# Keys and the second layer's first product from quarters, values ahead of the queries, channel sums in node order

## The chip, the core and the metric

The kernel runs on one core of a Trainium2 chip. The metric is the device time of one execution in microseconds (us): the median of several runs. Five engines work side by side[...]: TensorE multiplies matrices (PE in the profile, its weight loads PEld), VectorE (DVE) and ScalarE (ACT) do elementwise work, GpSimd (POOL) does some elementwise work and issues part of the DMAs, and SyncE (SP) issues the other DMAs. Each engine works through its own instructions in program order.

## The reference

Two layers over 16 graphs of N = 1024 nodes with C = 256 channels each, all in float32. `LN` is a layer normalisation over the channels.

```
# layer 0, per graph, h = relu(LN(x))
c      = mean over channels of h                         # one number per node
A      = | |sigmoid(c[m] - c[n]) - 0.5| - 0.5 | * 2      # N x N, symmetric
g      = relu((h^T @ (adj * A)) * para)                  # C x N
q      = g^T in 4 heads of 64;   k, v = h @ kv_w in 4 heads
x      = x + softmax(q k^T * scale) v
# layer 1, h = relu(LN(x))
agg    = D (adj + I) D h                                 # D from the degrees
y      = agg @ W1^T + b1                                 # 256 -> 512 channels
z      = relu(batchnorm(y)) @ W2^T + b2                  # batchnorm over all graphs and nodes
x      = x + batchnorm(z)
```

The first batch norm needs `y` of all graphs, so the kernel has two phases: everything up to `y` graph by graph, with `y` stored in DRAM, and after that the second product and the second batch norm.

## The kernel before

**Layout.** Channels or nodes lie on the 128 partitions. N is 8 tiles of 128 (`NT`), C is 2 (`CC`), the 512 channels of `y` are 4 (`HC`), and a product writes 128 x 512 (`FB`). `product` (lines 167 to 171) makes one 128 x 128 by 128 x 512 product from two matmuls with 64 columns each, which the trace shows as four records. It is the line L171 of queries, keys, values, aggregate and `hidden` alike, which differ by the tile they write: `pg`, `pk`, `pv`, `pa`, `py`.

**Attention sets the beat.** `attention` (from line 1092) walks through 16 graphs, 4 units each (two pairs of heads, two halves of the queries), 4 steps per unit: 256 steps. A step issues the scores of two key tiles (`sc`, L933), their exponentials (`p`, L941, ScalarE), the additions of `p` for the softmax's denominator (`acc`, L962 and L965, VectorE) and the products with the values (`o`, L976) of the step before. When a unit ends, VectorE transposes `o` (L990), GpSimd writes it to `out_d` (L994), SP reads it back (`gather`, L1000), VectorE folds `acc` (L1011, L1012), and a few steps later `add_output` (L1074, L1082) scales the result and adds it to `xs[b]`, the residual.

**The background.** Between the steps, `background(b)` hands out the other graphs' work in pieces. Each piece yields its TensorE time in us; `attention` takes pieces until the sum reaches `due`, a share of `total` that grows evenly over the graph's 16 steps. While graph b attends, the background makes, in this order: keys and values of graph b+1 (`keys_values`: 8 products of keys from `ht`, copied out by ScalarE at L660, then 4 banks of values, copied out at L677); the queries of b+1 (`queries`, seven products of quarters in place of eight, with `weigh` making the weights, and `normed(b-1)` the second norm of the graph before, which ends with `load_x(b + 2)` for its freed buffer); the aggregate of b-1 (`aggregate`, again seven products of quarters), with the first norm of b+2 beside it; and `hidden(b-1)`: 8 blocks of two products each, biased and copied by ScalarE (L773), written to DRAM by GpSimd (L774), their statistics taken by VectorE (L777). `prepare(b+2)` weaves into `hidden` the transposed copy of graph b+2's `h` (`squares` on VectorE, written to `hsq_d`, read back by `gathered`) and the first weights. An action given to `soon` is issued with the next piece.

**Seven for eight.** `queries`, `aggregate` and the second phase use a scheme for 2 x 2 blocks that takes seven products and 15 block additions. The second operand's combinations in order are t1 = b12 - b11, t2 = b22 - t1, t3 = b22 - b12, t4 = b21 - t2; the first's are s1 = a21 + a22, s2 = s1 - a11, s3 = a11 - a21, s4 = a12 - s2.

**Buffers.** Products of the background share three PSUM banks in rotation (`ps_mm`, through `bank`); `o` has one bank, `sc` two tiles. Pool `p4` has four buffers of `p`, `p3` three each of `x`, `ht` and `adj`, `p2` two of `h`, `p8` eight weights, `py` four of `y`.

**Channel sums.** `weigh` needs c for every node twice: per partition (`csum`) and along the row (`cbc`, the same row on all partitions). `differences` (from line 428) writes `csum` to `csum_d` and reads it back to all partitions. For graph 0 and 1 the row is in node order. From graph 2 on it is written as it lies, (partition, tile), and `weigh` reads it with a step of 8 elements: `cbc.rearrange("p (q t) -> p t q", t=NT)`. The reader is L485, `w<-cbc,csum`.

**The degrees' row.** `load_later` (lines 290 to 297), called once in graph 1's background, loads W1, writes `dinv` to `dinv_d` (L294) and reads it back to all partitions as `dbc` (L295); `aggregate` scales with it.

Of the kernel before, what the change touches and what calls it, by code (L numbers as in the profile page):

```python
# [10 lines left out]
F32 = mybir.dt.float32  # L11
# [12 lines left out]
def gnn_two_layers_kernel(  # L24
# [34 lines left out]
    vec = const.tile([P, 18], F32, name="vec")  # L59
    nc.sync.dma_start(out=vec, in_=vecs)  # L60
    b1, g1, be1 = (vec[:, i * HC : (i + 1) * HC] for i in range(3))
    b2, g2, be2 = (vec[:, 3 * HC + i * CC : 3 * HC + (i + 1) * CC] for i in range(3))
# [34 lines left out]
    def layers(shifted):  # L97
# [13 lines left out]
        py = st.enter_context(tc.tile_pool(name=f"py_{kind}", bufs=4))  # L111
# [7 lines left out]

        xs, hs, hts, ats, qs, ks, vs = {}, {}, {}, {}, {}, {}, {}  # L120
        invs = {}
        csums, cbcs, weighted, weighers = {}, {}, {}, {}
# [50 lines left out]
        def load_x(b):  # L173
            xs[b] = p3.tile([P, NT, C], F32, tag="x", name=f"x_{b}")
            parts = 4 if b == 0 else 2
            for part in range(parts):
                t = slice(part * NT // parts, (part + 1) * NT // parts)
                nc.sync.dma_start(
                    out=xs[b][:, t], in_=x[b].rearrange("(t p) c -> p t c", p=P)[:, t]
                )  # L180
# [108 lines left out]

        def load_later():  # L290
            later["w1"] = big.tile([P, CC, H1], F32, tag="w1", name="w1")
            nc.sync.dma_start(out=later["w1"], in_=w1_t.rearrange("(k p) j -> p k j", p=P))
            later["dbc"] = const.tile([P, N], F32, tag="dbc", name=f"dbc_{kind}")
# [5 lines left out]
        class Norm:  # L299
# [3 lines left out]
            def __init__(self, b, first):  # L303
                tag = "a" if first else "b"
                self.src = xs[b]
# [4 lines left out]
                if first:  # L310
                    self.csum = p2.tile([P, NT], F32, tag="csum", name=f"csum_{b}")
                    csums[b] = self.csum
                self.h = p2.tile([P, NT, C], F32, tag="h", name=f"h_{tag}_{b}")
# [114 lines left out]
        def differences(b):  # L428
# [4 lines left out]
            cbcs[b] = (  # L433
                cbc.rearrange("p (t q) -> p t q", t=NT)
                if b <= 1
                else cbc.rearrange("p (q t) -> p t q", t=NT)
            )
# [4 lines left out]
            if b == 1:  # L442
                turned = bank(f"csumt_{b}")[0:NT, 0:P]
                nc.tensor.transpose(turned, csums[b], ident)
                row = p1.tile([P, NT // 2, P], F32, tag="s1", name=f"csumr_{b}")[0:NT, 0, :]
                nc.scalar.copy(row, turned)
                nc.sync.dma_start(out=csum_d[b].rearrange("(t p) -> t p", p=P), in_=row)
            else:
                nc.sync.dma_start(out=csum_d[b].rearrange("(p t) -> p t", p=P), in_=csums[b])
# [199 lines left out]
        def keys_values(b):  # L649
            ht = hts[b]  # L650
            ks[b] = [p4.tile([P, N], F32, tag="k", name=f"k_{b}_{k}") for k in range(CC)]
            for g in range(NH):
                for j in range(CC):
# [7 lines left out]
                    yield 1.71  # L661

            vs[b] = [p4.tile([P, NT, P], F32, tag="v", name=f"v_{b}_{k}") for k in range(CC)]
# [18 lines left out]
        def aggregate(b):  # L682
# [3 lines left out]
            order = (0, 2, 5, 1, 4, 6, 3)  # L686
# [35 lines left out]
            def sixth(m):  # L722
                add(c21, m, c21)
                soon(lambda: scale(c21, 0))
# [5 lines left out]
            for i, (left, after) in enumerate(  # L730
# [5 lines left out]
                    (None, fifth),  # L736
                    (a22, sixth),
                    (a12, seventh),
# [4 lines left out]
                for th in range(NP // 2):  # L743
# [9 lines left out]
                    elif i == 0:  # L753
                        combine("b", b, nc.vector)
                    yield 1.71

        def hidden(b):

# [31 lines left out]
        def normed(b):  # L790
# [4 lines left out]
            if b + 3 < B:  # L795
                load_x(b + 3)
# [15 lines left out]
        def prepare(b, products):  # L812
# [4 lines left out]
            if b == 2:  # L817
                for k in range(CC):
                    yield from weave(islice(products, 3), (0, islice(w, AHEAD // 2)))
                    yield TOP  # L820
                    transposed(b, (k,))
                    yield 1.0
# [741 lines left out]
```

## Time and profile before

| what | us |
|---|---|
| median of 3 runs | 2489.23 (2488.91 to 2490.34) |
| the profiled execution | 2488.76 |
| its span | 2487.0 |
| granted TensorE clock over the span | 0.993 |

An engine's "busy" is the union of its instructions' times. "x" gives how many there were. In a row of windows, the first numbers are the stretch from the span's start, its length, and then each engine's busy time with the instructions in brackets; at the end come the granted TensorE clock, the share that the DMA engines were busy, and GB/s. A row of waits names the instruction that waited, what released it, the total in us, how often, and the longest. In a timeline a row has its start, its length, the engine, the line, the operation, out<-in with shapes, and how many in a row; in brackets is the idle time ahead of it. The rows of the groups that the change concerns:

```profile
L485 ACT ACTIVATE w<-cbc,csum 128x512 f32<-128x512 f32 x256 | 285.8, 1168 | 0.0
L171 PE MATMUL py<-at,w 128*64 128x512 f32 x1024 | 228.4, 592 | 0.2 <-ACT y L773 0.2
L773 ACT ACTIVATE y<-py,vec 128x512 f32<-128x512 f32 x128 | 87.4, 683 | 115.4 <-PE py L171 91.8
L171 PE MATMUL pk<-ht,kvw_f 128*64 128x512 f32 x512 | 115.2, 592 | 0.2 <-ACT ht L404 0.2
```

The stages: until about 75 us the first graph's own preparation, until 2160 the attention with its background, until 2214 the last aggregate and `hidden`, then the second phase.

### The profile page before, as it was taken

The page shows a single profiled execution, that of the slowest core. Times are in us where ns is not written, and L with a number is a line of the kernel's source. Part 1 is how long each engine was busy: PE and PEld are TensorE (multiplying, and loading weights), DVE is VectorE, ACT ScalarE, POOL GpSimd, SP SyncE. Part 2 cuts the span into 40 slices and gives each one's busy share as a digit, 9 for nine tenths or more (in the row PEclk, how much of TensorE's full clock was granted, in tenths as well). Part 3 has the DMA queues.
Part 4 walks back from the last instruction along what each step waited for, and adds up shares of the span by engine and source line. Part 5 has one row for each costly group of instructions (what it writes and reads, how often), then busy time and mean ns, then how long its engine had stood idle before and what let it go on. Part 6 is the DMA issues. An engine that isn't in the chain of part 4 may idle for free. (4 is left out here: it accounts for less than half of the span.)

```text
span 2487.0 us, 35569 instructions
## 1 busy us (share of the span) xinstructions
PE 2435.7 (98%) x13403; PEld 841.2 (34%) x13403; DVE 1882.0 (76%) x2920; ACT 1401.7 (56%) x1927; POOL 429.2 (17%) x527
## 2 busy tenths in 40 slices
PE   9999999999999999999999999999999999999995
PEld 4333333333333333333333333333333332334444
DVE  5668787877778787878787787868787877767775
ACT  7775564647473746656474747465564634345544
POOL 1640101010101001011101010110101001036652
PEclk9999999999999999999999999999999999999997
DMA  4754535354545545362645445543536344355559
GB/s 150 238 173 172 170 114 199 101 199 129 197 145 178 164 159 169 116 206 84 215 126 182 145 174 169 178 153 132 191 94 210 116 140 162 132 214 220 189 199 374
DMA packets 187909, 421.42 MB, mean 169 GB/s; under 512 B 21832, under 2 KB 81744, under 8 KB 181968
## 3 DMA queue, kind: packets, MB, share of 16 engines
q1 hardware_dynamic: 158560, 311.56, 37.9%
q0 software_dynamic: 29168, 107.50, 11.6%
q8 instruction: 108, 1.77, 0.3%
q14 instruction: 73, 0.60, 0.1%
HBM read 315.63 MB, written 103.35 MB: 168 GB/s over the span
## 5 line engine op out<-in xcount | busy, mean ns | idle before, releaser
L941 ACT ACTIVATE p<-sc 128x1024 f32<-128x1024 f32 x512 | 494.9, 1019 | 617.6 <-PE sc L933 617.2
L965 DVE TENSOR_TENSOR acc<-acc,p 128x1024 f32<-128x1024 f32 x384 | 471.3, 1227 | 165.1 <-ACT p L941 143.8
L933 PE MATMUL sc<-q,k 64*64 64x512 f32 x4096 | 498.8, 602 | 6.2 <-ACT p L941 6.2
L976 PE MATMUL o<-p,v 128*64 128x512 f32 x2048 | 494.5, 604 | 0.3 <-DVE os L990 0.3
L171 PE MATMUL pg<-w,h_a 128*64 128x512 f32 x1600 | 359.8, 592 | 0.8 <-DVE w L472 0.8
L171 PE MATMUL pa<-aht,h_b 128*64 128x512 f32 x1536 | 346.0, 592 | 1.1 <-ACT h_b L342 1.0
L485 ACT ACTIVATE w<-cbc,csum 128x512 f32<-128x512 f32 x256 | 285.8, 1168 | 0.0
L933 PEld LDWEIGHTS sc<-q,k 64*64 64x64 f32 x4096 | 131.0, 132 | 347.9 <-issue 286.5
L472 DVE SCALAR_TENSOR_TENSOR w<-w,adj 128x1024 f32<-128x1024 f32 x128 | 156.9, 1225 | 95.0 <-ACT w L493 91.1
L171 PE MATMUL py<-at,w 128*64 128x512 f32 x1024 | 228.4, 592 | 0.2 <-ACT y L773 0.2
L976 PEld LDWEIGHTS o<-p,v 128*64 128x64 f32 x2048 | 124.4, 136 | 298.3 <-issue 260.3
L994 POOL DMA_DIRECT2D out_d<-os x58 | 34.2, 590 | 1070.8 <-DVE os L990 1037.5
L171 PEld LDWEIGHTS pg<-w,h_a 128*64 128x64 f32 x1600 | 114.8, 137 | 229.2 <-issue 218.8
L171 PEld LDWEIGHTS pa<-aht,h_b 128*64 128x64 f32 x1536 | 109.9, 137 | 215.3 <-issue 202.0
L773 ACT ACTIVATE y<-py,vec 128x512 f32<-128x512 f32 x128 | 87.4, 683 | 115.4 <-PE py L171 91.8
L493 ACT ACTIVATE w<-w 128x1024 f32<-128x1024 f32 x128 | 135.1, 1055 | 1.7
L774 POOL DMA_DIRECT2D y_d<-y x128 | 69.7, 545 | 371.8 <-ACT y L773 362.6
L548 DVE TENSOR_TENSOR w<-w,w 128x1024 f32<-128x1024 f32 x112 | 132.7, 1214 | 1.5
L171 PEld LDWEIGHTS py<-at,w 128*64 128x64 f32 x1024 | 74.0, 137 | 145.5 <-issue 131.5
L171 PE MATMUL pv<-kvw_f,ht 128*64 128x256 f32 x1024 | 116.1, 379 | 0.0
L171 PE MATMUL pk<-ht,kvw_f 128*64 128x512 f32 x512 | 115.2, 592 | 0.2 <-ACT ht L404 0.2
L342 ACT ACTIVATE h_b<-x,lnsm_b 128x256 f32<-128x256 f32 x128 | 69.9, 599 | 65.9 <-DVE lnsm_b L331 65.9
(169 smaller groups left out, 2665.4 us busy)
## 6 DMA issues: line engine op xcount, KB each, us to landing
aht<-aht_d SPq DMA_DIRECT2D x224, 512.0 KB, 6.4
adj<-in_adj_dram SPq DMA_DIRECT2D x128, 512.0 KB, 4.8
y_d<-y POOLq DMA_DIRECT2D x128, 256.0 KB, 3.0
yin_f<-y_d SPq DMA_DIRECT2D x32, 1024.0 KB, 6.4
para<-in_para_dram SPq DMA_DIRECT2D x64, 256.0 KB, 3.6
x_d<-x POOLq DMA_DIRECT2D x16, 1024.0 KB, 5.2
xo_f<-x_d SPq DMA_DIRECT2D x32, 512.0 KB, 8.2
out_dram<-xo_f POOLq DMA_DIRECT2D x32, 512.0 KB, 10.8
```

Source lines behind the costliest of these rows:

```text
L171: nc.tensor.matmul(dst[r], left[:, r], right, start=start, stop=stop)
L342: nc.scalar.activation(self.h[:, t, :], self.src[:, t, :], AF.Relu, bias=self.sm[:, 1, t : t + 1], scale=self.sm[:, 0, t : t + 1], accum_o ...
L472: nc.vector.scalar_tensor_tensor(w, w, 1.0, a, op0=ALU.add, op1=ALU.mult)
L485: nc.scalar.activation(w[:, t, :].rearrange("p (t q) -> p t q", q=P), cbc[:, q * NT // NH : (q + 1) * NT // NH], AF.Abs, bias=csum[:, th * ...
L493: nc.scalar.activation(made[i], made[i], AF.Tanh, scale=-0.5 / C)
L548: nc.vector.tensor_sub(block(i)[part], block(x)[part], block(y)[part])
L773: nc.scalar.activation(y, made, AF.Identity, bias=b1[:, j : j + 1])
L774: nc.gpsimd.dma_start(out=y1_d[i][:, j, :], in_=y)
L933: nc.tensor.matmul(sc[part, e, :], ks[b][k][r, m * P + c * HW : m * P + (c + 1) * HW], qs[b][k][r, f * FB : (f + 1) * FB], start=True, sto ...
L941: nc.scalar.activation(pr, sc, AF.Exp)
L965: nc.vector.tensor_add(self.acc, self.acc, pr)
L976: nc.tensor.matmul(self.o[r, :], vs[b][k][:, m, r], pr[:, e, :], start=(m == 0), stop=(m == NT - 1),)
```

## The change

- **Keys** of graphs 3 to 15 are made by seven products (`keys_of`). `key_steps` makes t1, t2, t3 on GpSimd (t3 in place of b12); t4 goes in place of b21. Two of the seven results are copied by ScalarE, five are added by VectorE, and two additions of finished blocks are made by GpSimd. The combined key weights are made once, in `load_later`.
- **Order.** For those graphs the values come first, in the place where keys and values stood, and the keys after the queries, ahead of the aggregate. `key_steps` is issued when twelve of the queries' fourteen pieces are.
- **`hidden`** of graphs 0 to 13 makes two halves of seven products. Four results go through ScalarE; ten are added by VectorE straight from PSUM; GpSimd makes t3 and t4 and four additions; t1 and t2 are made by VectorE at the end of the aggregate. Graphs 14 and 15 keep the old form (`plain_hidden`). The aggregate's last two products change places, so that the quarters that `hidden` needs first are ready.
- **Channel sums.** VectorE transposes `csum` in blocks of 32, and four DMAs write it in node order, for every graph from 1 on; `cbc` is then always read in order.
- **x** is loaded twice: once into a buffer of `h`, where the first norm works in place (`load_x(b, True)`), and once as the residual into a single buffer, when the second norm of the graph before has read it (`load_x(b + 1)` in `normed`).
- `py` has six buffers; `total`, the waits of a graph's first unit (6 for 5) and the pieces of `prepare` are set to the new counts. The new function `combined` stands in the middle of the old `load_later`, so that the lines which make `dbc` now belong to `combined`, and it is called twice.

```diff
+        def w1_quarters():
+            HH = H1 // 2
+            return [later["w1"][:, k, m * HH : (m + 1) * HH] for m in (0, 1) for k in (0, 1)]
+
         def load_later():
             later["w1"] = big.tile([P, CC, H1], F32, tag="w1", name="w1")
             nc.sync.dma_start(out=later["w1"], in_=w1_t.rearrange("(k p) j -> p k j", p=P))
+            later["kvs"] = kvs = p1.tile([P, 4, P], F32, tag="kvs", name=f"kvs_{kind}")
+            combined(kvs, key_weights())
+            later["s"] = big.tile([P, 4, H1 // 2], F32, name="w1s")
+            combined(later["s"], w1_quarters())
+
+        def combined(into, quarters):
+            s1, s2, s3, s4 = (into[:, i] for i in range(4))
+            a11, a12, a21, a22 = quarters
+            nc.gpsimd.tensor_add(s1, a21, a22)
+            nc.gpsimd.tensor_sub(s2, s1, a11)
+            nc.gpsimd.tensor_sub(s3, a11, a21)
+            nc.gpsimd.tensor_sub(s4, a12, s2)
             later["dbc"] = const.tile([P, N], F32, tag="dbc", name=f"dbc_{kind}")
             nc.sync.dma_start(out=dinv_d.rearrange("(t p) -> p t", p=P), in_=dinv)
             nc.sync.dma_start(
...
-            if b == 1:
-                turned = bank(f"csumt_{b}")[0:NT, 0:P]
-                nc.tensor.transpose(turned, csums[b], ident)
...
-            else:
-                nc.sync.dma_start(out=csum_d[b].rearrange("(p t) -> p t", p=P), in_=csums[b])
+            turned = p1.tile([P, SQ], F32, tag="csumt", name=f"csumt_{b}")
+            nc.vector.transpose(turned, wides[b])
+            for i in range(NS):
+                nc.sync.dma_start(
+                    out=csum_d[b].rearrange("(t i s) -> i t s", i=NS, s=SQ)[i],
+                    in_=turned[i * SQ : i * SQ + NT],
+                )
...
+        def key_steps(b):
+            b11, b12, _, b22 = blocks(hts[b])
...
+            nc.gpsimd.tensor_sub(t1, b12, b11)
+            nc.gpsimd.tensor_sub(t2, b22, t1)
+            nc.gpsimd.tensor_sub(b12, b22, b12)
...
+        def keys_of(b):
...
+            def second(m):
+                add(c11, m, c12)
+                nc.gpsimd.tensor_sub(b21, b21, t2)
+
+            def fifth(m):
+                add(c21, m, c12)
+                nc.gpsimd.tensor_add(c12, c12, c22)
+                nc.gpsimd.tensor_add(c22, c22, c21)
+
+            for i, (left, right, after) in enumerate(
+                (
+                    (a11, b11, lambda m: nc.scalar.copy(c12, m)),
+                    (a12, b21, second),
+                    (s1, t1, lambda m: nc.scalar.copy(c22, m)),
+                    (s2, t2, lambda m: add(c12, m, c12)),
+                    (s3, b12, fifth),
+                    (s4, b22, lambda m: add(c12, m, c12)),
+                    (a22, b21, lambda m: add(c21, m, c21)),
+                )
+            ):
+                made = bank(f"pk_{b}_{i}")
+                product(made, left, right, True, True)
+                after(made)
+                yield 0.86
...
         def hidden(b):
+            if b >= B - 2:
+                yield from plain_hidden(b)
+                return
...
+            def m1(c):
+                part = one("1", a11, c, b11)
+                nc.scalar.activation(
+                    new("11", c), part, AF.Identity, bias=b1[:, c : c + 1]
+                )
+
+            def m2(c):
+                y = made["11"]
+                add(y, one("2", a12, c, b21), y)
+                put(y, 0, c)
+
+            def m3(c):
+                y = made["12"]
+                add(y, one("3", s4, c, b22), y)
+                put(y, 1, c)
...
+            def m7(c):
+                part, y = one("7", s3, c, t3), made["22"]
+                nc.vector.scalar_tensor_tensor(
+                    new("sum", c), part, b1_step[:, c : c + 1], made["21"], op0=ALU.add, op1=ALU.add
+                )
+                nc.gpsimd.tensor_add(y, y, made["sum"])
+                put(y, 1, 2 + c)
+
+            for c, order in ((0, (m1, m5, m6, m2, m3, m7, m4)), (1, (m1, m6, m2, m5, m7, m3, m4))):
+                for each in order:
+                    each(c)
+                    yield 0.86
...
             yield from Norm(b, False).all()
-            if b + 3 < B:
-                load_x(b + 3)
+            load_x(b + 1)
...
-                yield from weave(queries(b + 1), (0, double(w)), (9, islice(norm, 5)))
+                asked = queries(b + 1)
+                yield from weave(islice(asked, 12), (0, double(w)), (9, islice(norm, 3)))
+                if b > 1:
+                    key_steps(b + 1)
+                yield from weave(asked, (0, islice(norm, 2)))
                 yield next(gather)
+                if b + 2 < B:
+                    load_x(b + 2, True)
                 yield from weave(products, (0, norm))
```

## The prediction

> **What bounds the kernel now.** I read the page's busy shares first, then the waits of TensorE, then a table of windows over the attention steps of one graph, then the rows of the operations concerned.
>
> ```profile
> PE 2435.7 (98%) x13403; PEld 841.2 (34%) x13403; DVE 1882.0 (76%) x2920; ACT 1401.7 (56%) x1927; POOL 429.2 (17%) x527
> ```
>
> ```profile
> PE o L976 <- DVE os L990: 0.3, 1, 0.3
> ```
>
> The second fence is the whole list of TensorE's waits between 240 and 2120 us: 0.3 us in 1880. So over thirteen graphs TensorE is the bound, and what is taken from it is gained unless something else becomes late. How close the others are is seen from one graph (its period is 1119.87 to 1254, 134 us), one row for one attention step:
>
> ```profile
> core 0: us, PE busy (x) PEld busy (x) DVE busy (x) ACT busy (x) POOL busy (x), PEclk, DMA share, GB/s
> 1119.87:1128.76 8.89, 8.89 (x50) 2.72 (x48) 6.11 (x9) 5.97 (x9) 1.08 (x2) 1.00 0.42 131
> 1128.76:1137.66 8.90, 8.90 (x51) 2.72 (x49) 6.68 (x8) 8.81 (x10) 0.00 (x0) 1.00 0.33 107
> 1137.66:1146.55 8.89, 8.89 (x50) 2.72 (x48) 6.35 (x7) 8.83 (x11) 0.00 (x0) 1.00 0.41 120
> 1146.55:1155.57 9.02, 9.02 (x55) 2.83 (x53) 8.81 (x13) 4.61 (x5) 0.00 (x0) 1.00 0.08 30
> 1155.57:1162.74 7.17, 7.17 (x42) 2.14 (x40) 7.14 (x11) 1.94 (x2) 0.00 (x0) 1.00 0.01 2
> 1162.74:1171.64 8.90, 8.90 (x51) 2.73 (x49) 8.76 (x14) 1.94 (x2) 1.45 (x2) 1.00 0.42 147
> 1171.64:1180.55 8.91, 8.91 (x66) 3.87 (x64) 8.84 (x24) 5.14 (x9) 3.17 (x4) 1.00 0.11 35
> ```
>
> ScalarE is full in steps 1 and 2 (8.8 of 8.9 us), VectorE is full in steps 3 to 6, 34 us on end, and TensorE never waits for it, but with little to spare: the timeline has `q<-pg` of the last query product ending at 1183.4, and the product that needs its bank next starts at 1184.2.
>
> [...] So I price a product by spacing, not by duration. [...] here VectorE adds two SBUF tensors of 512 elements in 2.67 us while GpSimd works, against 0.69 elsewhere:
>
> ```profile
> 2227.45 2.35 POOL L1327 TENSOR_TENSOR t_f<-yin_f,yin_f 128x1024 f32<-128x1024 f32 x1
> 2227.67 2.67 DVE L1382 TENSOR_TENSOR y_f<-y_f,y_f 128x512 f32<-128x512 f32 x1
> ```
>
> [...] GpSimd's 128x256 subtraction took 0.98 us, its 128x1024 one 2.36, so I take 1.4 us for 128x512, an estimate between these rows.
>
> **TensorE.** The chain of waits has
>
> ```profile
> 2181.94 17.39 PE pa L171 x80
> 2199.33 13.57 PE py L171 x63
> ```
>
> 80 records in 17.39 us. The last drains for about 0.38, so (17.39 - 0.38)/79 = 0.215 us each, and a product of 128x128 by 128x512 has four of them: 0.86 us. Keys: 8 products become 7, for graphs 3 to 15: 13 x 0.86 = 11.2. `hidden`: 16 become 2 x 7 = 14, for graphs 0 to 13: 28 x 0.86 = 24.1. The transpose of graph 1's channel sums goes (0.3). Together **35.6 us** off. Aggregate, queries, values and attention keep their products, and the second phase (2214 to 2487) is untouched.
>
> **ScalarE.** The row L485 takes 1232 ns from graph 2 on, where `cbc` is read with a stride, and 715 in the first 75 us, where it is read in order. The change makes all of them ordered: 16 x 0.52 = 8.3 us less per graph, all before step 3. Six evacuations per graph (two of `k`, four of `y`, about 0.6 each) leave as well. ScalarE is off the bound, but steps 1 and 2 hand their exponentials over earlier: VectorE waited 2.29 us for one at 1144.5. That is worth nothing by itself and gives VectorE about 2 us of lead into its full stretch.
>
> **VectorE.** Added per graph: 5 adds of `k`, 10 of `y`, 2 in `steps_of`: 17 at 0.65 (spacing; 0.69 duration) = 11.1 us, and a small transpose. It has 104.3 busy in 133 us, so it goes to 115.4 of 130.4, 88%. On average it fits. Locally there are three places.
> (1) `hidden`. Its last two steps now have 9.7 and 10.5 us of VectorE rows against 8.0 and 8.2 of TensorE. I laid the products on the three rotating banks by hand: attention 3.64 us per step, then products every 0.86; each evacuation in VectorE's order (pair of `acc` 2.40, statistics 0.62, add 0.65, weighting 1.14). All are in time but one: the second half's m3 needs the bank of m2, which is added after the step's two `acc`, 0.65 late. 14 x 0.65 = 9.1 us.
> (2) Keys. They come where the values stood, right behind the full stretch, and want VectorE where the values wanted ScalarE. Product 2 needs the bank of the last query product 1.7 us earlier than now, with 0.8 to spare now; the 2 us of lead cover it, and the three GpSimd subtractions of `key_steps`[...] use the rest. Product 6 needs the bank of product 3, which waits behind two `acc`: 0.6 late. 13 x 0.6 = 7.8 us. VectorE's own waits for the two GpSimd adds of `fifth` (2 x 1.4) fall in front of an attention stretch of 3.64 and cost nothing.
> (3) The single `o` bank: the next unit's first value product waits for VectorE's transpose of the last. At the start of a graph VectorE is some 3 us behind, and 3.9 are left by the same layout: nothing.
>
> **DMA and queues.** x is read twice: 16 MB more on 421 (a share of about half the engines): nothing. The residual x lands in a single buffer only after the last `h_b`; it is issued at step 7 to 8, 5.6 us to landing, first added at the end of step 9: hidden. On SP it stands where `load_x(b + 3)` stood. The second half of `ht` is gathered after the second half's m2, four issues of 0.5 and 4.0 us to landing against 3.4 us of products and 3.64 of attention: 1.2 us to spare at the median, late by about 1 at the longest landing (6.2): nothing, 0 to 1 us a graph in the range. GpSimd has 12 more operations a graph; `out_d` queues behind them, with two steps to spare.
> One thing is not hidden. The load of `dbc` now sits in `combined`, which `load_later` calls twice, so SP issues `dinv_d`, `dbc`, `dinv_d`, `dbc`, each waiting for the one before. Today:
>
> ```profile
> SPq L295 <- DMA dinv_d<-deg: 10.4, 1, 10.4
> ```
>
> ```profile
> 185.48 0.34 SPq L295 DMA_DIRECT2D dbc_f<-dinv_d  x1
> 185.87 0.43 SPq L528 DMA_DIRECT2D para<-in_para_dram  x1
> 186.39 1.38 SPq L184 DMA_DIRECT2D adj<-in_adj_dram  x2
> ```
>
> ```profile
> 195.79 1.22 DVE L472 SCALAR_TENSOR_TENSOR w<-w,adj 128x1024 f32<-128x1024 f32 x1
> ```
>
> The second pair holds SP for about 4.5 (the like broadcast `cbc`) + 11.0 = 15.5 us. Behind it is graph 2's `adj` tile for the weighting at 195.79, landed at 191.2 today (4.8 after issue): 4.6 are cover, 10.9 stall VectorE, in front of its `acc` and of a bank that TensorE wants at about 200. I take **9 us** once; 0 to 13 in the range.
>
> **Sum.** -35.6 + 9.1 + 7.8 + 9 = -9.7 us. The profiled execution took 2488.76 (span 2487.0, 1.8 around it), so 2479.1; the median of the runs is 0.5 above it: **2479**.
>
> **Rivals.**
> A, the sum above: small late banks in `hidden` and keys. For: VectorE's steps with no room. Against: 0.6 us is within what a layout by hand can know; slack won at one stall covers the next. Chance 0.43, own range 2468 to 2489.
> B, the stalls vanish: ScalarE's 8.3 us a graph put VectorE ahead, and only the single SP block or nothing is left: 2453.6 to 2463. For: full VectorE steps hid behind TensorE before. Against: it gains 11 us of work. Chance 0.33.
> C, VectorE becomes the bound. Its 115.4 us a graph[...] make 132.2, against TensorE's 130.4; with 2 us of waits it can't avoid, 134.2, 1.2 longer than today's 133. Thirteen graphs: +16, and +9 for SP: 2514. It decides from a mean stall of (35.6 - 9)/13.5 = 2.0 us a graph. For: steps 3 to 6 are full already, and key steps and keys land at their end. [...] Chance 0.24.
> That the products aren't saved can be left out: the changed kernel's instruction order has 7 and 14 of them.
>
> **How the numbers follow.** A measurement of this kernel can tell about 0.2% (5 us) from no change, so faster is below 2484.2. A gives faster 0.33 and same 0.10; B faster 0.33; C same 0.04 and slower 0.20. Faster 0.66, same 0.14, slower 0.20. The range 2456 to 2500 leaves out the best part of B (about 0.07) and the worse half of C (0.12).
>
> **What would show it.** Right: TensorE's waits name VectorE's adds of `y` and `k` ahead of products, 0.5 to 1 us each, some 27 of them; one gap of about 9 us near 200; L485's successor at about 715 ns; the period 131 to 132 us. B: no waits between 240 and 2080, period 130.4. C: VectorE over 95% busy in every graph, adds of 1.8 us and more beside GpSimd, period over 133. The forecast is wrong in kind if waits for `x`, `ht` or `aht` transfers lead the list.

## The result, and the profile after

The changed kernel takes 2551.7 us (median of 4 runs, 2550.6 to 2553.7) against 2489.1 for the kernel before on the same chip: a ratio of 1.0251 with the interval 1.0238 to 1.0264. It is slower by 62.6 us, where 9.7 fewer were forecast. From the page of the changed kernel, the span, the busy shares, and the row that answers to L485 before:

```profile
span 2548.4 us, 36085 instructions
PE 2431.4 (95%) x13238; PEld 824.9 (32%) x13238; DVE 2072.0 (81%) x3168; ACT 1247.0 (49%) x1844; POOL 667.6 (26%) x714
L512 ACT ACTIVATE w<-cbc,csum 128x512 f32<-128x512 f32 x256 | 170.6, 719 | 4.5 <-DMA cbc<-csum_d 4.5
```

TensorE has 165 records fewer and is 95% busy instead of 98. Each piece of the differences |c[m] - c[n]| costs 719 ns instead of a mean of 1168, close to the 715 forecast. VectorE is at 81%, so it is not full on average. Where TensorE waits is in its list of waits, 240 to 2180 us (waiting instruction, releaser, total, times, longest):

```profile
PE pk L174 <- DVE k L727: 18.7, 12, 1.7
PE pk L174 <- ACT k L739: 14.3, 12, 1.2
PE py L174 <- DVE y L907: 7.5, 13, 0.6
PE pk L174 <- DVE k L740: 5.3, 8, 0.8
PE py L174 <- DVE y_sum L936: 2.2, 13, 0.2
```

Four more rows are of one wait each, 0.5 to 0.7 us. Before, the list from 240 to 2120 us was 0.3 us long. Three of the five rows belong to the keys (`pk`), up to 12 times each: the keys of graphs 3 to 14. The hidden products (`py`) have the two others.

The place is one attention step in each graph. Stretches of the changed kernel: the step with the keys in three graphs, and one step after it.

```profile
core 0: us, PE busy (x) PEld busy (x) DVE busy (x) ACT busy (x) POOL busy (x), PEclk, DMA share, GB/s
1077.60:1090.01 12.41, 8.84 (x47) 2.22 (x46) 10.02 (x16) 7.70 (x13) 3.37 (x4) 1.00 0.73 262
1216.62:1228.99 12.37, 8.82 (x46) 2.22 (x44) 10.03 (x16) 7.70 (x13) 3.36 (x4) 1.00 0.71 261
936.60:949.97 13.37, 10.55 (x48) 2.42 (x46) 10.01 (x16) 7.70 (x13) 4.28 (x4) 0.82 0.75 270
949.97:960.00 10.03, 10.03 (x57) 3.13 (x55) 6.71 (x12) 2.59 (x3) 2.19 (x4) 0.90 1.07 374
```

The step takes 12.3 to 13.4 us, and TensorE is busy for 8.8 of them at full clock. In the longer ones the granted clock is below 1: the stall costs a second time, which is taken up with the first experiment. In its timeline, of which only VectorE, ScalarE and TensorE are shown, the scores start at 1077.60:

```profile
1079.32 1.26 DVE L561 TENSOR_TENSOR q<-q,para 128x512 f32<-128x512 f32 x2
...
1080.50 0.68 DVE L609 TENSOR_TENSOR q<-pg,q 128x512 f32<-128x512 f32 x1
...
1081.33 1.94 PE L174 MATMUL pk<-kt,kvs_f 128*64 128x512 f32 x8
1081.51 1.24 DVE L360 TENSOR_TENSOR lnsm_b<-lnsm_b,deg 128x4 f32<-128x4 f32 x1 [0.33 <-POOL lnsm_b L97]
...
1084.01 0.68 DVE L727 TENSOR_TENSOR k<-pk,k 128x512 f32<-128x512 f32 x1
1084.12 0.63 ACT L563 ACTIVATE q<-q 128x512 f32<-128x512 f32 x1
1084.66 1.92 ACT L1138 ACTIVATE p<-sc 128x1024 f32<-128x1024 f32 x2
1084.84 1.08 PE L174 MATMUL pk<-ht,kvs_f 128*64 128x512 f32 x4 [1.57 <-DVE k L727]
1085.69 2.55 DVE L1162 TENSOR_TENSOR acc<-acc,p 128x1024 f32<-128x1024 f32 x2 [1.01 <-ACT p L1138]
1086.46 0.59 ACT L739 COPY k<-pk 128x512 f32<-128x512 f32 x1
...
1087.10 1.08 PE L174 MATMUL pk<-ht,kvs_f 128*64 128x512 f32 x4 [1.19 <-ACT k L739]
...
1088.16 0.68 DVE L740 TENSOR_TENSOR k<-pk,k 128x512 f32<-128x512 f32 x1
...
1088.99 1.08 PE L174 MATMUL pk<-ht,kvw_f 128*64 128x512 f32 x4 [0.81 <-DVE k L740]
```

Key products are counted from 1 here (the prediction counted them from 0, and in the expectations a waiting product is counted from 0 and an emptied one from 1). With three banks in rotation product 5 needs the bank of product 2, 6 that of 3, 7 that of 4. The row at 1081.33 is products 3 and 4. L727 empties the bank of product 2, which ended at about 1077.7. It stands on VectorE behind the last query block (L609, L561, with a wait of 0.45 us for its parameter tile) and a tiny operation of the second norm (L360) that takes 1.24 us. The exponentials (L1138) begin 7.1 us after their scores, because ScalarE first finishes the query and norm pieces, some of which wait for VectorE in their turn. Behind them wait ScalarE's copy of product 3 (L739) and, through the two accumulations (L1162), VectorE's addition of product 4 (L740). TensorE's last three products wait 1.57, 1.19 and 0.81 us for these banks.

Once, in graph 1, another thing is late. From VectorE's list of waits of the changed kernel:

```profile
DVE w L499 <- DMA adj<-in_adj_dram: 20.3, 2, 19.4
```

SyncE's queue and VectorE at that moment:

```profile
187.38 0.34 SPq L321 DMA_DIRECT2D dbc_f<-dinv_d  x1
191.90 0.36 SPq L320 DMA_DIRECT2D dinv_d<-deg  x1
200.80 0.33 SPq L321 DMA_DIRECT2D dbc_f<-dinv_d  x1
201.18 0.43 SPq L555 DMA_DIRECT2D para<-in_para_dram  x1
201.72 1.96 SPq L192 DMA_DIRECT2D adj<-in_adj_dram  x2
```

```profile
209.42 1.23 DVE L499 SCALAR_TENSOR_TENSOR w<-w,adj 128x1024 f32<-128x1024 f32 x1 [19.42 <-DMA adj<-in_adj_dram]
```

### The profile page after: what moved, and what is told of

Read it like the earlier page. It is cut to its first block, busy times and chain, and to the rows that moved or that the text cites. A ratio compares the mean times of both kernels' runs of the same rounds, so it can differ in the third digit from the quotient of the medians.

```text
span 2548.4 us, 36085 instructions
## 1 busy us (share of the span) xinstructions
PE 2431.4 (95%) x13238; PEld 824.9 (32%) x13238; DVE 2072.0 (81%) x3168; ACT 1247.0 (49%) x1844; POOL 667.6 (26%) x714
## 3 DMA queue, kind: packets, MB, share of 16 engines
q0 software_dynamic: 29168, 107.50, 11.2%
## 5 line engine op out<-in xcount | busy, mean ns | idle before, releaser
L1138 ACT ACTIVATE p<-sc 128x1024 f32<-128x1024 f32 x512 | 495.6, 1019 | 643.2 <-PE sc L1130 643.0
L1162 DVE TENSOR_TENSOR acc<-acc,p 128x1024 f32<-128x1024 f32 x384 | 484.1, 1261 | 94.0 <-ACT p L1138 73.1
L174 PE MATMUL pg<-w,x_h 128*64 128x512 f32 x1472 | 333.8, 595 | 16.6 <-DVE x_h L585 16.6
L499 DVE SCALAR_TENSOR_TENSOR w<-w,adj 128x1024 f32<-128x1024 f32 x128 | 166.7, 1310 | 45.3 <-ACT w L520 24.9
L174 PEld LDWEIGHTS pg<-w,x_h 128*64 128x64 f32 x1472 | 106.0, 138 | 222.1 <-issue 209.1
L512 ACT ACTIVATE w<-cbc,csum 128x512 f32<-128x512 f32 x256 | 170.6, 719 | 4.5 <-DMA cbc<-csum_d 4.5
L520 ACT ACTIVATE w<-w 128x1024 f32<-128x1024 f32 x128 | 136.0, 1063 | 2.5
L174 PE MATMUL py<-at,w1s 128*64 128x512 f32 x448 | 109.5, 598 | 9.7 <-DVE y L907 7.5
L174 PE MATMUL py<-at,w 128*64 128x512 f32 x464 | 113.9, 595 | 1.4 <-DVE at L797 0.7
L563 ACT ACTIVATE q<-q 128x512 f32<-128x512 f32 x56 | 34.9, 630 | 162.0 <-DVE q L561 161.3
L1159 DVE TENSOR_TENSOR acc<-p,p 128x1024 f32<-128x1024 f32 x64 | 78.8, 1232 | 30.6 <-ACT p L1138 30.5
L1502 ACT ACTIVATE yin_f<-yin_f,sm_f 128x512 f32<-128x512 f32 x128 | 93.6, 803 | 16.2 <-DMA yin_f<-y_d 16.0
```

What stands on the lines that cost most here:

```text
L174: nc.tensor.matmul(dst[r], left[:, r], right, start=start, stop=stop)
L499: nc.vector.scalar_tensor_tensor(w, w, 1.0, a, op0=ALU.add, op1=ALU.mult)
L512: nc.scalar.activation(w[:, t, :].rearrange("p (t q) -> p t q", q=P), cbc[:, q * NT // NH : (q + 1) * NT // NH], AF.Abs, bias=csum[:, th * ...
L520: nc.scalar.activation(made[i], made[i], AF.Tanh, scale=-0.5 / C)
L1138: nc.scalar.activation(pr, sc, AF.Exp)
L1159: nc.vector.tensor_add(self.acc, self.held, pr)
```

## The experiments

Times are medians. Every run has its own comparison with the kernel before, which lay between 2488.9 and 2489.3 us. None of these kernels changes what is computed. Theory 1 was the one read off the trace above: the keys stand in the wrong place, behind the query tail. Theory 2 is that VectorE has too much work wherever it stands, and theory 3 that GpSimd's operations hold VectorE up (L360's 1.24 us above stand beside one of 1.27, L728).

**e1_dbc: the degree row once.**

```diff
         def combined(into, quarters):
...
             nc.gpsimd.tensor_sub(s4, a12, s2)
-            later["dbc"] = const.tile([P, N], F32, tag="dbc", name=f"dbc_{kind}")
-            nc.sync.dma_start(out=dinv_d.rearrange("(t p) -> p t", p=P), in_=dinv)
-            nc.sync.dma_start(
...
```

(The lines go into `load_later`, right behind the load of W1 and so ahead of the weights' sums, not after them as the expectation has it.)

> The changed kernel with the two transfers of the degree row (row out, row back in to all partitions) issued once, after the weights' sums, instead of once inside each of the two calls that form the sums. Computation unchanged. In the trace of the changed kernel graph 1 takes 155.6 us against 136.6 before, and VectorE waits once for 19.4 us for an adjacency transfer. If the second issue of the degree row blocks SyncE's queue (my term, 9 us, range 0 to 13), the time falls by 17 to 20 us, to about 2533, and that 19.4 us wait is gone. If the loss in graph 1 is the weights' sums on GpSimd instead, the time falls by under 5.

2534.7 us, 17.0 less than the changed kernel. The wait of 19.4 us is down to 3.4:

```profile
DVE w L499 <- DMA adj<-in_adj_dram: 4.1, 2, 3.4
```

The sums of the weights on GpSimd are still there, so they were not the loss. The term is settled, at nearly twice my size for it. All later kernels have this edit.

This run also shows TensorE's clock behind such a stall. Stretches of 2 us in one key step of e1_dbc:

```profile
1066.90:1068.90 2.00, 0.94 (x4) 0.23 (x4) 0.99 (x3) 2.00 (x4) 0.00 (x0) 1.00 0.92 344
1068.90:1070.90 2.00, 0.81 (x4) 0.30 (x4) 1.90 (x2) 2.00 (x4) 0.00 (x0) 0.65 1.00 401
1070.90:1072.90 2.00, 2.00 (x6) 0.32 (x4) 1.77 (x3) 0.26 (x1) 0.00 (x0) 0.50 1.00 394
1072.90:1074.90 2.00, 2.00 (x8) 0.31 (x8) 0.68 (x1) 0.00 (x0) 1.90 (x2) 0.50 1.09 362
1074.90:1076.90 2.00, 2.00 (x16) 0.50 (x8) 0.70 (x2) 0.76 (x1) 0.63 (x1) 0.65 1.09 347
```

In the second stretch, at 1069.48, the granted clock goes from 1.00 to 0.50, by these rows for about 6.8 us, and TensorE works off the rest of the keys and most of the next scores at that clock. What this costs a product is seen in the changed kernel: the four records of a restarted key product take 1.08 us at full clock (943.89) and 1.98 at 0.50 (946.16). In that kernel's trace the clock falls seven times between 230 and 2150 us, each time to 0.50 and for 3.41 or 6.83 us, and the falls lie multiples of 3.41 us apart. So I look at stretches of that length, laid so that each fall is the end of one. Two of e1_dbc, each in a key step:

```profile
1066.07:1069.48 3.41, 1.50 (x6) 0.23 (x4) 2.06 (x4) 3.27 (x5) 0.00 (x0) 1.00 0.93 348
1209.40:1212.80 3.40, 1.67 (x8) 0.20 (x4) 2.93 (x3) 2.71 (x5) 0.00 (x0) 1.00 1.02 417
```

In the first TensorE is busy for 44%, and the clock falls at its end; in the second for 49%, and it does not. Between 230 and 2150 us of the changed kernel's trace TensorE is busy for 32 to 45% of the seven stretches that a fall ends, and for 47% or more of every other:

```profile
1361.66:1365.07 3.41, 1.08 (x4) 0.23 (x4) 2.40 (x3) 3.26 (x6) 0.00 (x0) 1.00 0.97 381
941.82:945.23 3.41, 1.52 (x7) 0.23 (x4) 1.89 (x4) 3.14 (x5) 0.00 (x0) 1.00 1.01 399
1225.12:1228.54 3.42, 1.62 (x8) 0.42 (x8) 3.21 (x4) 1.92 (x4) 0.00 (x0) 1.00 1.02 407
```

The first two are the least and the most busy of the seven, the third is the least busy of the others. So in this trace the busy share of such a stretch goes with the fall, and not the length of one gap: the longest wait is 1.57 us in the key step shown above, which keeps its clock, and 1.63 in the one whose clock falls at 945.23. Of the changed kernel's 12 key steps, five kept a clock of 1.00 and took 12.26 to 12.41 us; seven had 0.82 to 0.95 and took 13.08 to 13.37, and after two of these the next step was longer too (10.03 and 10.05 for 9.01). By this estimate the clock makes 7 x 0.9 + 2 x 1.0 = 8 us of the loss.

**e2_oldkeys, e3_plainhid: which of the two products.** e2 takes the keys back to their old form and place; e3 takes the second layer's product back and leaves the keys.

```diff
# e2_oldkeys
-            if b > 2:
+            if False:
                 yield from values_of(b)
                 yield from keys_of(b)
# e3_plainhid
-            if b >= B - 2:
+            if True:
                 yield from plain_hidden(b)
```

(with the steps, `total` and the pieces of `prepare` that belong to each form)

> As e1_dbc, with all keys formed as before the change: 8 plain products ahead of the values, no steps on GpSimd. Theory 1 (the keys from quarters stand behind the query tail and the second norm, and their products wait for evacuations that VectorE and ScalarE's queues hold back): the stall of 4.3 to 5.4 us in each of 12 graphs goes, 12 x 4.9 = 59 us, and 13 x 0.86 = 11 us of TensorE work come back: about 2485. Theory 2 (VectorE has too little left after 11 us more work in each graph, wherever it stands): the keys are only about half of that extra work, so about half of the stall stays and shows up in the hidden products: 2510 or more.

> As e1_dbc, with the second layer's first product plain in all graphs (16 products a graph with ScalarE evacuations, its weave as before the change); keys from quarters stay. Theory 1: the stall at the keys is local and stays, 4.3 to 5.4 us a graph; the hidden products give back 14 x 1.7 = 24 us of TensorE work less 14 x 1.4 = 20 us of their own stalls: within 8 us of e1_dbc. Theory 2 (VectorE as a whole): about 6 us of VectorE work a graph gone, so the keys' stall falls to under half: 25 us or more below e1_dbc.

e2: 2481.8 us, ratio 0.9970 (0.9958 to 0.9981): the whole key stall goes, and with it 52.9 us. e3: 2579.5, 44.8 above e1_dbc, which neither theory had. With VectorE at 76% it is the slowest of all, so the amount of VectorE work does not decide. Its key stall has one wait of 5 us:

```profile
PE pk L174 <- DVE lnsm_b L360: 60.7, 12, 5.1
```

With the other number of hidden products and the `total` that goes with it, product 3 of the keys now falls just ahead of an attention step. It needs the bank of the last query product, and in the trace that bank's addition (L609, 1228.49) stands behind a pair of accumulations of 3.59 us (1224.98).

**e4_front, e5_plainafter: place or form.** e4 puts the keys from quarters at the front of the graph, right behind the values. e5 leaves them in the changed place, but makes them plainly.

```diff
# e4_front
                 yield from weave(islice(products, 4), (0, islice(w, 4)))
                 if b == 1:
                     load_later()
+                if b > 1:
+                    key_steps(b + 1)
+                    yield from weave(products, (0, islice(w, 4)))
                 asked = queries(b + 1)
...
# e5_plainafter
             if b > 2:
                 yield from values_of(b)
-                yield from keys_of(b)
-                return
...
```

> As e1_dbc, with the keys' steps and seven products moved to the front of the graph, straight after the values and ahead of the queries; same arithmetic, same operations. Theory 1 (place): the query tail and the second norm no longer stand ahead of the keys' evacuations, the stall falls from 4.3 to 5.4 us to 0 to 2.5 us a graph: 30 to 59 us below e1_dbc, 2475 to 2505. Theory 2 (amount of VectorE work): the same work in another place, within 10 us of e1_dbc. Theory 3[...]: the same 9 GpSimd operations, so also near e1_dbc.

> As e1_dbc, in the changed order (values ahead of the queries, keys between the queries and the aggregate), but the keys formed plainly: 8 products of 2 x 512 columns, each pair of them left by one ScalarE copy; no GpSimd steps, no VectorE adds. If the place alone makes the stall (every bank there waits behind the query tail and the exponentials): still 3 us or more of stall a graph, 2515 or more. If it is the place together with the form (product 4, 5, 6 each need a bank that VectorE or ScalarE lets go within 1.7 us): no stall, as e2_oldkeys, 2478 to 2488.

e4: 2543.7, 9.0 above e1_dbc: the number that theories 2 and 3 gave, but not for their reason. The key stall fell, to one wait of 1.5 us a graph, but the aggregate, which now follows the queries at once, waits for its input:

```profile
PE pa L174 <- DMA aht<-aht_d: 32.1, 20, 2.4
PE pk L174 <- DVE k L740: 18.0, 12, 1.5
```

So what stands between queries and aggregate is also the cover of the aggregate's first loads. e5: 2481.6, the same as with the keys in the old place, and no wait of a `pk` at all. The place does no harm by itself: plain keys, left by ScalarE, are free there. Theory 1 as I had put it falls; it is this form in this place.

**e6_dve: the steps on VectorE.**

```diff
-            nc.gpsimd.tensor_sub(t1, b12, b11)
+            nc.vector.tensor_sub(t1, b12, b11)
```

(and t2, t3, t4 likewise)

> As e1_dbc, with the four sums that prepare the keys (three steps and the fourth one after product 2) on VectorE instead of GpSimd: 4 x 0.69 = 2.8 us more of VectorE work a graph[...]. Theory 3 (GpSimd's holds): the pair of accumulations goes from 3.5 back to 2.5 us and the small operations of the norm from 1.2 to 0.2, so 1 to 2 us of the stall go: 12 to 24 us below e1_dbc's 2534.7. Theory 1 (order in the queues): VectorE reaches the evacuations later by 2.8 less 1 to 2: 0 to 20 us above e1_dbc. Theory 2 (amount): 20 to 35 above.

2539.8, 5.2 above e1_dbc, with waits of 17.8 for L727 and 15.4 for L739 as before. In its timeline (a step near 1062) the pair of accumulations takes 2.54 (3.54 in the changed kernel) and L360 0.16, as theory 3 says, and still L727 starts no sooner: the steps on VectorE and a wait of 1.65 for the parameter tile fill the time. A new row appears too, 9.3 us in 13 waits for L609, the last query block. So 2.8 us more of VectorE work a graph, with the holds gone, cost 0.4 net. The run changes amount and holds against each other and cannot price either alone; the forecasts of theory 2 and of theory 3 both missed, and the number lies where theory 1 put it.

**e7_swap, e8_mixed: other orders.** e7 has the keys from quarters at the front and the values in the middle. e8 alternates them in both places (part of its edit):

```diff
+                made = {"k": keys_of(b), "v": values_of(b)}
+                for each in "vkvkkvkkvkk":
+                    yield from islice(made[each], 1)
```

> As e1_dbc, but the keys from quarters stand at the front of the graph and the values between the queries and the aggregate, with the third step in a buffer of its own and the fourth in the second's, so that the values find their input whole; the steps are formed at the end of the graph before. e4_front showed two things: the stall at the keys fell to about 2 us a graph there, and the aggregate waited 32 us in all for its input, since nothing stood between it and the queries. Here the values give that cover back. Theory 1: 12 x 2 us of stall or less and no wait for the aggregate's input: 2475 to 2505. If the evacuations collide at the front as much as in the middle (right behind the hidden products' own adds): 2525 or more.

> As e1_dbc, with keys from quarters and values alternating: value, key, value, key ahead of the queries, then key, value, key, key, value, key, key between the queries and the aggregate; the steps in buffers of their own, formed at the start of the graph. Same products and evacuations as e1_dbc, so the same VectorE work. A value product takes 1.71 us and is left by ScalarE, so most key evacuations have 2.6 us instead of 1.7 before their bank is asked for. Theory 1 (order and deadlines): most of the stall goes, 0.5 to 2 us a graph left: 2475 to 2500. Theory 2 (amount): within 15 us of e1_dbc.

Theory 1 missed both times: 2562.6 and 2549.9, 27.9 and 15.2 above e1_dbc. For e7 the other branch of the expectation came true, a collision at the front; for e8 the number is near theory 2's limit of 15. Each has one long wait a graph, about which theory 2 says nothing:

```profile
PE pk L174 <- DVE k L728: 53.4, 13, 4.1
```

```profile
PE pk L174 <- DVE lnsm_b L360: 50.4, 12, 4.5
```

(e7 first.) In e8 the timeline of one such step has, on VectorE:

```profile
1207.75 3.29 DVE L1166 TENSOR_TENSOR acc<-acc,p 128x1024 f32<-128x1024 f32 x2
1210.96 0.68 DVE L609 TENSOR_TENSOR q<-pg,q 128x512 f32<-128x512 f32 x1
```

The last query product had ended at 1205.1; its addition stood in the queue behind two accumulations, as in e3. In e7 product 2's addition (L728 there) stands behind an accumulation of 2.29, a transpose and a weighting (1018.7 to 1022.6). So theory 4, from e3, e7 and e8: `attention` writes a step's accumulations ahead of the background's evacuations, wherever the background's products stand; what decides is the order on VectorE within a step. Alternating the products gave the evacuations more time, but what stood ahead of them was longer still.

**e9_late, e10_late_dve: evacuations first.** In the step with key products 3 to 7 the accumulations are written last; e10 also lets VectorE, not ScalarE, copy product 3.

```diff
+                late = s < len(steps) and b > 1 and s % per_graph == 7
-                if s < len(steps):
+                if s < len(steps) and not late:
                     for pr in made:
                         unit.add(pr)
...
                     done += cost
+                if late:
+                    for pr in made:
+                        unit.add(pr)
# e10_late_dve also
-                    (s1, t1, lambda m: nc.scalar.copy(c22, m)),
+                    (s1, t1, lambda m: nc.vector.tensor_copy(c22, m)),
```

> As e1_dbc, but in the one step of each graph that holds key products 3 to 7, the two accumulations of the step's exponentials are written after the products' evacuations instead of ahead of them on VectorE. Same work. Theory 4, formed on e7 and e8 (the order on VectorE: every evacuation of a step stands behind the accumulations, these behind the exponentials, and these behind what ScalarE has in its queue): product 4 no longer waits for L727, but product 5 still waits for ScalarE's copy of product 3, which stands behind the exponentials; product 6 comes about 1 us sooner. So 1 to 2 us of the 4.9 go, and some of the halved clock: 12 to 30 us below e1_dbc, 2505 to 2522. If VectorE's amount of work is what counts: within 8 us of e1_dbc.

> As e9_late, with product 3 left by VectorE instead of ScalarE too, so that no evacuation of the step stands behind the exponentials: VectorE has 0.1 us more work a graph, not less. Theory 4: what is left is the query tail (the last query block's wait for its parameter transfer, 0.45 us, and the norm's small operations), under 1.5 us a graph, and the clock is no longer halved after it: 45 to 60 us below e1_dbc, 2475 to 2490. Theory 2 (amount): within 10 us of e1_dbc.

e9: 2527.4, 7.3 less than e1_dbc: under the 12 to 30 that I expected, and a number that theory 2 (within 8) would allow. L727 still costs 18.3 us (it stands behind the query tail, not behind this pair), and L739 14.7; only the row of L740 is gone. e10: 2494.4, 40.3 less than e1_dbc, although VectorE has one copy of 0.68 us more in each graph (the 0.1 in the expectation was wrong). That is less than the 45 to 60 I expected, but it rules theory 2 out. Turning the order round brought 7.3, the copy on top of it 33.0 (the copy alone was not run), part of which is the clock (a mean of 0.986 in e9, 0.992 in e10). Of the keys' waits one row that recurs is left:

```profile
PE pk L174 <- DVE k L727: 18.7, 12, 1.7
```

and the key step takes 9.5 to 10.1 us, in place of e1_dbc's 12.3 to 13.5.

**e11_tail to e15_neither: what is left, and the other parts.** e11 starts the last norm pieces two key products later and gives the last parameter tile a buffer of its own. e12 writes the accumulations last in step 15 too. e13 moves one more norm piece. e14 is e2 with step 15 mended; e15 has neither product from quarters.

```diff
# e11_tail
-                yield from weave(products, (0, norm))
+                yield from weave(products, (2 if b > 1 else 0, norm))
...
# e12_tail_hidden
-                late = s < len(steps) and b > 1 and s % per_graph == 7
+                late = s < len(steps) and b > 1 and s % per_graph in (7, 15)
# e13_norm_late
-                yield from weave(asked, (0, islice(norm, 2)))
+                yield from weave(asked, (0, islice(norm, 1)))
```

> As e10_late_dve, with what still stands ahead of product 2's evacuation moved: the last four pieces of the second norm start two key products later, and the last query block's parameter tile has a buffer of its own, loaded two query products earlier. In e10_late_dve TensorE still waits 1.5 us a graph for L727, behind the norm's small operation (1.24 us) and a 0.45 us wait for the parameters. Theory 4: that wait goes: 12 x 1.5 = 18 us below e10_late_dve's 2494.4, 2474 to 2480, so below the kernel before and below e2_oldkeys. If L727 is late for another reason (VectorE busy with the accumulation before it): under 5 us of it go.

> As e11_tail, with the accumulations written behind the evacuations also in the last step of a graph, in which the second layer's products 2, 5, 7, 3 and 4 of the second half run. In every run so far TensorE waits 13 x 0.57 us there for the addition of product 2 (L907), which stands behind the accumulations. Theory 4: these 7.5 us go: 5 to 9 us below e11_tail. If the later accumulations push the front of the next graph instead: 0 to 10 us above it.

> As e12_tail_hidden, with one more piece of the second norm (its fifth: the multiplication of 128x4 that takes 1.23 us beside a GpSimd subtraction, and two ScalarE passes) moved behind the key products 1 and 2. If that operation, held by GpSimd, is what product 2's evacuation stands behind: the 1.0 us a graph goes, 12 us below e12_tail_hidden's 2481.0, about 2469, with period 134 us. If VectorE is late there anyway, or the aggregate now waits for the norm's output: within 4 us of e12_tail_hidden.

> As e2_oldkeys (plain keys in their old place, second layer's product from quarters), with the accumulations of a graph's last step written behind the evacuations. TensorE waits 13 x 0.57 us there for L907 in e2_oldkeys. The wait goes: 5 to 9 us below e2_oldkeys' 2481.8, 2473 to 2477. If not, within 3 us.

> As e1_dbc with neither product from quarters: plain keys in the old place, plain second layer's product. What is left of the change is the channel sums in node order, the features loaded twice, the order of the aggregate's last two products and the weights made at other moments. I put these at nothing together with an end of the first graph that is 2 to 3 us shorter: 2484 to 2490. Above 2492 or below 2482 one of them has a price of its own.

e11: 2488.2, 6.1 less than e10, a third of what I expected; product 2's addition (L729 there) still made TensorE wait 1.0 us a graph, behind L360. e12: 2481.0, another 7.2 less, in the middle of what was expected: the wait for the addition of m2 in the second half (L909 there) falls from 13 times to one. e13: **2465.5 us, ratio 0.9902 (0.9887 to 0.9917)**, 15.6 less than e12, some 3 more than expected. It is the fastest here, and has all of the change in it. Its list of TensorE's waits begins with

```profile
PE py L174 <- DVE y_sum L938: 2.2, 13, 0.2
PE pa L174 <- ACT h_b L374: 2.1, 2, 1.2
PE py L174 <- DVE group L1232: 0.7, 1, 0.7
```

and its key step is full, 8.15 us in place of 12.3 to 13.4, with a clock of 1.00:

```profile
900.93:909.08 8.15, 8.15 (x46) 2.60 (x45) 7.01 (x15) 5.53 (x10) 4.32 (x4) 1.00 0.01 3
```

In graph 1 it still loses time: VectorE waits 6.4 us for the adjacency tile, and TensorE 4.3 behind it.

The piece that e13 moves contains L360, a multiplication of 128x4, which takes 1.23 us in e12 beside a GpSimd subtraction of 1.26 us (L730) and 0.15 in e13, where it starts as that subtraction ends. But e13 moves the piece's two ScalarE passes and its wait for GpSimd's result too, so what L360's shorter time alone is worth was not measured.

e14: 2471.7, 10.1 less than e2, just beyond the 5 to 9 expected. e15: 2490.4, ratio 1.0005 (0.9996 to 1.0013), 0.4 above the range expected: the channel sums, the second load of x and the new order of the rest are together worth nothing that these runs can tell.

## Why the prediction was wrong

Four of the runs make a chain from the kernel before to the changed one, one part at a time:

| part | from, to | forecast us | measured us |
|---|---|---|---|
| channel sums, x twice, orders | before, e15 | -0.3 | +1.3 |
| second layer's first product | e15, e2 | -24.1 + 9.1 = -15.0 | -8.6 |
| keys from quarters, values ahead | e2, e1 | -11.2 + 7.8 = -3.4 | +52.9 |
| degree row twice | e1, changed | +9 | +17.0 |
| sum | | -9.7 | +62.6 |

The parts do not simply add. With the second layer's product plain, the keys from quarters cost 89.1 us (e15 to e3) and not 52.9, and with the keys from quarters in place the second layer's product gives 44.8 us (e3 to e1) and not 8.6. What the keys cost depends on where the rest makes them fall within a step.

**The step that failed is "(2) Keys".** What it says of one bank holds: "Product 6 needs the bank of product 3, which waits behind two `acc`: 0.6 late" is the row of L740, 0.81 in the step shown. What it leaves out is the two products ahead of that one. It puts ScalarE's queue at nothing: the exponentials of that step come 7.1 us behind their scores, since the query and norm pieces of that moment stand ahead of them, so the copy of product 3 is 1.19 late. And it puts nothing ahead of product 2's addition, where VectorE has the query tail and the norm: that is 1.57 late. The three were priced at 0.6 and are 3.6. The three restarted products take 1.08 us each where running ones are 0.86 apart, 0.7 more. That makes the 4.1 to 4.3 us between a key step of the changed kernel at full clock and one of e13; the halved clock adds up to 1.1 in the step and, twice, 1.0 in the next. As an estimate from the changed kernel's trace, 12 x 4.2 + 8 = 58 us were lost where 7.8 were forecast. What the form saves without these waits is seen from e14 to e13, 6.2 us, where 11.2 were forecast; 58 less 6 comes near the 52.9 measured. That it is the order and not the work is shown by e10 (40.3 less, with more work on VectorE) and e13 (all the work, and 1% faster than before).

**The sentence on the bank of the last query product** ("2 us of lead cover it, and the three GpSimd subtractions of `key_steps` ... use the rest") held in all graphs but one: the bank's row (L609) is a single wait of 0.7 us. But it was close: e6 had it late by 0.7 in every graph, and e3 and e8, which changed the products around it, by 4 to 5.

**Hidden**: the late bank was named rightly (m3 of the second half, for the bank of m2, behind the two accumulations) and sized rightly: 9.1 forecast, 7.5 in the list of waits; when it was removed, 10.1 came back from e2 to e14 and 7.2 from e11 to e12. What else is missing from the 15.0 is partly the short waits for L936 (2.2); some 3 us, within the uncertainty of that difference, stay unexplained.

**The degree row**: right mechanism, and the term mis-sized: 17.0 for 9. I had put the second pair at 15.5 us on SP; between the two reads it is 13.4 (187.38 to 200.80). The error is in the cover. I subtracted the 4.6 us by which the adjacency tile had lain ready before VectorE used it at 195.79. That was not slack but VectorE's other work, and in the changed kernel VectorE arrives sooner: the weighting starts at 209.42 after a wait of 19.42, so VectorE was free for it at 190.0. Even with one pair (e1) it waits 3.4 for the tile.

**TensorE's savings** were real: the period of a graph is 136.0 us before and in e15, 134.0 in e13, 2.0 less of the 2.6 that three products of 0.86 make. I had written 134 for the period before, and reckoned with 133, which was a misreading.

**Rivals.** C ended on the right side, but not by its mechanism: VectorE is 84% busy in e13, the fastest, and 81% in the changed kernel. Its 132.2 us a graph are the 115.4 and 16.8 for 12 GpSimd operations, each put at up to 1.4 us of delay for VectorE, an estimate; in the changed kernel a pair of accumulations and L360 took 1.0 and 1.1 us longer beside such operations. Its threshold, a mean stall of 2.0 us a graph, was passed because of the order in the queues. What the prediction lacked was a rival for exactly that: a product moved behind a tail that fills two in-order queues.

## What to carry to other kernels

A product is not moved to a place, it is moved behind whatever the engines that empty its bank have queued at that moment: lay out each such engine's queue, from the wait at its head, and not only TensorE's own timetable. Where a loop writes its own elementwise work ahead of the background's evacuations, turn the two round in the steps in which a bank is wanted soon, and take the evacuation of such a bank from an engine whose queue holds it up: here the first alone brought 7.3 us, both together 40.3. A run of short waits can cost more than its sum: in 7 of the changed kernel's 12 key steps TensorE's clock went from 1.00 to 0.50 behind it.

## What was unexpected about the hardware

- No single wait of TensorE in the changed kernel's key steps was longer than 1.7 us; still the clock fell in 7 of 12 of them. Between 230 and 2150 us of its trace, in stretches of 3.41 us laid to end at the falls, it fell behind all seven in which TensorE was busy for 45% or less, and behind none with 47% or more.
- A VectorE multiplication of 128x4 took 1.24 us in the changed kernel's key step beside a GpSimd subtraction of 128x512 (1.27 us), and 0.16 in the step before; a pair of accumulations took 3.54 us beside such subtractions and 2.55 without. In e6_dve, with the subtractions on VectorE itself, the two took 0.16 and 2.54.
